# Four transformer blocks on one NeuronCore: the last block's cross attention scores issued three steps ahead, its exponentials placed behind weight copies

## The chip, the cores and the metric

One core of a Trainium2 chip runs the whole program in one launch. The metric is device time in microseconds; the time before is the median of three runs. The engines are TensorE (PE, with its weight loads shown as PEld), VectorE (DVE), ScalarE (ACT), GpSimd (POOL) and SyncE (SP, which issues the loads).

## What is computed

Eight sequences of 112 tokens of 256 features pass through four blocks; a context of 375 tokens of 192 features is shared by all cross attentions. Blocks L0 and L1 have self attention, cross attention and a gated feed-forward part, L2 has cross attention alone, L3 is a decoder layer. The last one matters most here (shortened):

```python
def _decoder_block(x, enc, tgt_mask, enc_mask, ...):   # 16 heads of 16 features
    h = _layernorm(x, ln1_w, ln1_b)
    qkv = (h @ qkv_w + qkv_b).reshape(B, T, 3, H, HD)
    attn = softmax(where(tgt_mask | causal, -inf, q @ k^T * scale))
    x = x + (attn @ v) @ proj_w + proj_b
    h = _layernorm(x, ln2_w, ln2_b)
    q, k, v = h @ q_w + q_b, enc @ k_w + k_b, enc @ v_w + v_b
    attn = softmax(where(enc_mask, -inf, q @ k^T * scale))
    x = x + (attn @ v) @ out_w + out_b
    h = gelu(_layernorm(x, ln3_w, ln3_b) @ mlp1_w + mlp1_b)
    return x + h @ mlp2_w + mlp2_b
```

Everything is float32. In L0 to L2 there are 16 heads of 64 features.

## The kernel before

**Stages and steps.** The ten parts of the four blocks are stages 0 to 9: 0 self, 1 cross, 2 feed-forward (L0); 3, 4, 5 the same (L1); 6 cross (L2); 7 self, 8 cross, 9 MLP (L3). Attention is cut into 176 *steps*, numbered in the order of execution. A self step takes eight heads of one sequence, a cross step four. Steps 0 to 47 are L0's, 48 to 95 L1's, 96 to 135 stage 6 with some steps of stage 7 between them. Stage 7 is woven in pairs of steps between sequences of stages 6 and 8 (132/133, 136/137, 142/143, 148/149 and 154/155 are the last pairs). Stage 8 starts at step 138; from 156 to 175 it runs without stage 7.

**A step's parts.** `add_step` makes these items for step s:

- `("S", s)`, `emit_s`: score matmuls into the PSUM pool `ps_s` (L986), and the first half of the softmax. `ps_s` has two tiles of two banks, and a step of stage 7 or 8 uses both. In stages 7 and 8 one DVE instruction per head adds the mask, takes the row extremum and moves the scores from PSUM to a probability tile `pr` (L934); an exponential per head follows on ACT in place (L942), with the row sum accumulated. In stages 1, 4 and 6 it is DVE maximum (L948), ACT exponential (L954), DVE reciprocal (L960) and a POOL multiply by the reciprocal per head (L963).
- `("E", s)`, `emit_late`, stages 7 and 8 only: the other half of the exponentials, kept in program order.
- `("T", s, k)`, `emit_t`: bank k of transposes of `pr` (L1013; three banks of four transposes in a cross step, two in a self step) into a tile of the PSUM pool `ps_m`, and its copy to a `wT` tile. In stages 7 and 8 the copy of bank 1 is on DVE (L1019), those of banks 0 and 2 on ACT (L1022). `ps_m` has four tiles in rotation, and every other matmul but the scores uses it too.
- `("PV", s)`, `emit_pv`: values (L1043) and their evacuation on DVE (L1054). They are issued for two steps at a time, every second iteration.
- for the last step of a sequence in stages 7 and 8, `("R", ...)` (reciprocal L1082, spread on POOL L1083) and `("N", ...)` (two transposes L1089, multiply L1091).

**Fillers.** All other work is planner items with a cost and a due time in steps: q/k projections of the last block (L725), values (L750), key jobs in two parts (`kj`: L791 begins them, L800 ends them), value jobs (`vj`: L866, L875 in the last block), output products with the next normalization (`norm`, L669), norm transposes (`hT`, L637), masks (`mask`, POOL), the last MLP's first product (`ff`, L1298) and its Gelu over a half of the result at a time (`gelu`, L1330). Projected q, k and v live in one SBUF tile, the *arena*, of 11300 columns; an item whose results find no room there waits. Weights come through a ring of seven buffers.

**Order.** TensorE's order is the order in which the items are issued. The main loop runs over iterations i: scores of step i+2, values (every second iteration), transposes of step i+1 with fillers between the banks, late exponentials of step i+2, fillers, and the first part of the next key or value job. On the other engines the instructions are ordered by a scheduler, except those that are marked `keep_in_program_order`. The interval of step n means the time from the start of its scores to the start of the scores of step n+1.

The main loop before:

```python
            if lo <= i + 2 < hi:
                plan.main(("S", i + 2))
            if lo <= i < hi:
                waiting.append(("PV", i))       # issued when two wait
            if lo <= i + 1 < hi:
                left -= plan.fill(2 * share, ...)
                for k in range(n):
                    plan.main(("T", i + 1, k))
                    left -= plan.fill(min(left, share))
            if ("E", i + 2) in plan.items and lo <= i + 2 < hi:
                plan.main(("E", i + 2))
```

Of the kernel before, what the change touches and what calls it, by code (L numbers as in the profile page):

```python
# [15 lines left out]
B, T, D = 8, 112, 256  # L16
S, DC = 375, 192
# [282 lines left out]
def kernel(ctx: ExitStack, tc: tile.TileContext, a: dict, out: bass.AP):  # L300
    nc = tc.nc
    PSUM = bass.MemoryType.PSUM
    RINGS = {"w": 7, "row": 2, "xn": 3}
    ARENA = 11300

    const = ctx.enter_context(tc.tile_pool(name="const", bufs=1))
    wpool = ctx.enter_context(tc.tile_pool(name="wpool", bufs=RINGS["w"]))
    rpool = ctx.enter_context(tc.tile_pool(name="rpool", bufs=RINGS["row"]))
    ppool = ctx.enter_context(tc.tile_pool(name="ppool", bufs=4))
    tpool = ctx.enter_context(tc.tile_pool(name="tpool", bufs=8))  # L310
    xpool = ctx.enter_context(tc.tile_pool(name="xpool", bufs=RINGS["xn"]))
    small = ctx.enter_context(tc.tile_pool(name="small", bufs=4))
# [8 lines left out]
    plan = Plan(RINGS, ARENA, lambda k: 512 if k[0] == "v" else S if k[0] == "k" and k[1] in (1, 4, 6, 8) else 4 * T)  # L321
# [7 lines left out]
    SEG = [0, 0, 0, 1, 1, 1, 2, 2, 2, 2]  # L329
# [216 lines left out]
    def add_masks():  # L546


        src = ("w", "m8")

        def load():
            m8 = wpool.tile([T, B * (T + S)], U8, tag="w", name="m8")
            nc.sync.dma_start(m8[:, : B * T], a["mask_BxS_bf0"].rearrange("b t -> (b t)").partition_broadcast(T))
            nc.sync.dma_start(m8[:, B * T :], a["mask_BxS2_bf0"].rearrange("b s -> (b s)").partition_broadcast(T))
            got[src] = m8

        def self_mask():
            nc.gpsimd.tensor_scalar_mul(cmask.rearrange("p b t -> p (b t)"), got[src][:, : B * T], NEG)
            nc.gpsimd.affine_select(
                cmask, cmask, pattern=[[0, B], [-1, T]], compare_op=ALU.is_ge, fill=NEG, base=0,  # L560
                channel_multiplier=1,
            )

        plan.add_load(Item(("load", "masks"), 0, load, makes=[src]))
        plan.add(Item(("mask", "self"), 0, self_mask, first_of(7, 0) - 8, uses=[src], seg=SEG[6]))
        yield
        for i in range(2):
            key = ("w", "cm", i)

            def place(i=i, key=key):  # L570
                got[key] = wpool.tile([T, 4, S], F32, tag="w", name="cm")

            plan.add_load(Item(("load", key), 0, place, makes=[key]))
            for n in range(4):

                def ctx_mask(i=i, n=n, key=key):
                    c = B * T + (4 * i + n) * S
                    nc.gpsimd.tensor_scalar_mul(got[key][:, n, :], got[src][:, c : c + S], NEG)

                b = 4 * i + n  # L580
                plan.add(Item(("mask", b), 0, ctx_mask, first_of(8, b) - 5, uses=[src, key], seg=SEG[7]))


    xns = {}
# [323 lines left out]
    steps = []  # L908
    at = {}
    norms = []  # L910
    bsums, pairs = {}, {}

    def add_step(st, b, blocks, dh, nk, qs, ks, qap, kap, vtile, mask, opos, ochunk, last=False, pair=None):

# [2 lines left out]
        s = len(steps)  # L917
# [3 lines left out]
        cell, late = {}, []  # L921
# [54 lines left out]
        def emit_s():  # L976
            if dh == 16 and (st, b) not in bsums:
                bsums[(st, b)] = small.tile([T, H], F32, tag="bsums", name="bsums")
            tiles = [ps_s.tile([T, 2, 512], F32, tag="s", name="s") for _ in blocks]

            order = [(i, n) for i, blk in enumerate(blocks) for n in range(len(blk))]
            if dh == 16:
                order.sort(key=lambda e: (e[1] // 2, e[0]))
            for i, n in order:
                h = blocks[i][n]
                nc.tensor.matmul(  # L986
                    tiles[i][:, n % 2, (n // 2) * nk : (n // 2 + 1) * nk], lhsT=qap(h), rhs=kap(h),
                    start=True, stop=True,
                )
            for i, blk in enumerate(blocks):  # L990
                pr = softmax(blk, tiles[i])
                for n, h in enumerate(blk):
                    cell[h] = pr[:, n % 2, n // 2, :]
            for _ in range(len(late) // 2):
                late.pop(0)()

        def emit_late():

            for exp in late:
                tc.keep_in_program_order(exp())  # L1000


        if nch == 1:
# [163 lines left out]
    def first_of(st, b):  # L1167
        return at[(st, b, 0)]
# [9 lines left out]
        return lambda t: [(("N", st, last_batch(t)), 1.2)]  # L1178

    def q_deadline(st, j):  # L1180
        return first_of(st, 2 * j) - 3.4

    L0 = ("L0_xattn_", "Wq1 Wk1 Wv1 Wo1 bo1 g1 b1 Wq2 Wk2 Wv2 Wo2 bo2 g2 b2 Wp Wf bf g3 b3 bp".split())
    L1 = (
# [24 lines left out]
    def hT_by(st):  # L1209
        if st == 9:  # L1210
            return lambda gi: last_of(8, last_batch(GROUPS[gi][-1])) + 2.0
        if st in ff_at:
            return lambda gi: ff_at[st] - 0.5 + 0.02 * gi
        return lambda gi: first_of(st, (256 * gi) // T) - 4

    def norm_by(st):
        f = hT_by(st)
# [19 lines left out]
    def cross_stage(st, wq, wk, wv, qscale, vscale):  # L1237
        last = st == 8
        for j in range(4):
            if last:  # L1240
                add_last_projection(st, "q", j, wq, ("sq", "qc"), q_deadline(st, j), 2)
            else:
                add_pair_projection(st, "q", j, wq, 4, lambda j, u: q_deadline(st, j) + 0.01 * u, qscale)
        for b in range(B):

            add_key_jobs(st, b, wk, lambda b, u: at[(st, b, u)] - 3.0, last)
            if not last:
                add_value_jobs(st, b, wv, lambda b, i: at[(st, b, (0, 0, 2)[i])] - 1.5 + 0.1 * i, vscale)

        if last:  # L1250
            add_last_values(st, wv, lambda b: first_of(st, b) - 1.3)
# [107 lines left out]
    st = 0  # L1359
# [82 lines left out]
    last_ff(9, w("m1"), L3 + "mlp1_b")  # L1442
    add_products(9, None, w("m2"), 8, after_last_ff(9), lambda t: f9 + 1 + 0.1 * t)


    plan.pump()
    for t in range(NT):
# [8 lines left out]
    nc.vector.tensor_copy(vcols, pt0[:, :NVR])  # L1456
    plan.now = 7.0

    cuts = [0, ff_at[2], ff_at[5], ff_at[9]]
    for seg in range(3):  # L1460
        lo, hi = cuts[seg], cuts[seg + 1]
# [14 lines left out]
        for i in range(lo - 2, hi):  # L1476
            plan.step = i
            left = plan.pace(i, seg)
            if i < lo:

                left = max(left, 6.5)
            plan.close_jobs()
            if lo <= i + 2 < hi:
                plan.main(("S", i + 2))


            if lo <= i < hi:
                waiting.append(("PV", i))
                full = 4 if seg < 2 and i < lo + 16 else 2
                if len(waiting) == full:  # L1490
                    while waiting:
                        plan.main(waiting.pop(0))
            if lo <= i + 1 < hi:
                n = steps[i + 1]
                share = left / (n + 2)
                left -= plan.fill(2 * share, 1.5 if i < lo else 0.0)
                for k in range(n):
                    plan.main(("T", i + 1, k))
                    left -= plan.fill(min(left, share))
            if ("E", i + 2) in plan.items and lo <= i + 2 < hi:  # L1500
                plan.main(("E", i + 2))
            plan.fill(left, 1.5 if i < lo else 0.0)


            plan.open_jobs(1 if i + 1 >= first_of(8, 0) or i + 2 in woven else 2, i + 3.5, seg)
# [38 lines left out]
```

## Time and profile before

| | |
|---|---|
| three runs | 1650.48, 1651.93, 1650.52 us; median 1650.52 |
| profiled execution | 1651.93 us, of which the span is 1650.1 |
| instructions in it | 30008 |
| mean granted TensorE clock | 0.999 |
| stage 8's first scores (step 138) | 1421.69 us |
| last scores (step 175) | 1597.85 us |
| last PE matmul starts | 1643.18 us |
| TensorE granted clock, 40 slices | 9 tenths or more in each |

Times are microseconds from the span's start. In rows of the timeline the columns are start, duration, engine, line, operation, output and inputs with their shapes, the number of instructions merged into the row, and in brackets how long the engine sat idle before it and what ended the wait. In the chain of waits a piece is start, duration, engine, tile and line. fp32 matmuls are recorded as two each: "x8" scores are four heads, "x48" values are two cross steps.

### The profile page before, as it was taken

Reading aid. Unit: us, or ns where it says so; the run is one execution under the profiler, and the core shown is the slowest. Engines: PE = TensorE matmul, PEld = TensorE weight load, DVE = VectorE, ACT = ScalarE, POOL = GpSimd, SP = SyncE. Lnnn points to the kernel's source line nnn. Section 1 sums busy time; section 2 is a strip of 40 time slices with the busy share of each in tenths; the row PEclk is TensorE's granted clock in tenths of the full one; section 3 lists DMA queues with packets and bytes.
Section 4 is the critical chain, followed back from the end, with each engine's and each line's share of the span. In section 5 each row is a group of like instructions: output and inputs, shape, how many; then the busy total and the mean of one; then the engine's idle time right before and its main releaser. Section 6 shows DMA issues by size and latency. Waiting matters only on the chain.

```text
span 1650.1 us, 30008 instructions
## 1 busy us (share of the span) xinstructions
PE 1631.5 (99%) x11772; PEld 1141.1 (69%) x11772; DVE 810.8 (49%) x2160; ACT 783.9 (48%) x2454; POOL 718.3 (44%) x687
## 2 busy tenths in 40 slices
PE   9999999999999999999999999999999999999999
PEld 8777766666657878666666665676666666766667
DVE  3544454545532244445444552345555556678762
ACT  3553444444531454434444452234445555777772
POOL 1323554655732223355565570364564447422110
PEclk9999999999999999999999999999999999999999
DMA  6020020000101011000000010100000000000000
GB/s 188 7 73 29 6 79 9 1 26 1 52 29 46 1 30 52 27 1 30 1 1 27 1 46 29 33 23 1 1 2 1 16 1 27 30 2 2 2 1 23
DMA packets 26611, 39.47 MB, mean 24 GB/s; under 512 B 1527, under 2 KB 21623, under 8 KB 26471
## 3 DMA queue, kind: packets, MB, share of 16 engines
q1 hardware_dynamic: 26231, 37.40, 7.2%
q8 instruction: 92, 1.51, 0.4%
q14 instruction: 48, 0.39, 0.1%
q10 hardware_dynamic: 240, 0.17, 0.0%
HBM read 35.88 MB, written 0.92 MB: 22 GB/s over the span
## 4 chain that ended last, share of the span: by engine, by line
PE 91%; ACT 3%; DVE 3%; POOL 1%; issue 1%; ACTq 0%; POOLq 0%; DVEq 0%
PE mm L669 13%; PE mm L703 11%; PE mm L1043 10%; PE s L986 10%; PE mm L1013 10%; PE mm L791 8%; PE mm L825 7%; PE mm L1263 6%; PE mm L800 5%; PE mm L834 4%; PE mm L750 3%; ACT pr L942 2%; PE mm L1298 2%; PE mm L637 1%; ACT pr L954 1%
## 5 line engine op out<-in xcount | busy, mean ns | idle before, releaser
L963 POOL TENSOR_SCALAR pr<-pr,rinv 112x375 f32<-112x375 f32 x384 | 468.7, 1239 | 331.9 <-DVE rinv L960 331.9
L954 ACT ACTIVATE pr<-s,nm 112x375 f32<-112x375 f32 (+1 forms) x640 | 301.9, 489 | 166.5 <-DVE nm L948 163.0
L355 DVE COPY arena<-mm 128x375 f32<-128x375 f32 (+4 forms) x187 | 112.4, 609 | 281.7 <-PE mm L800 138.3
L1013 PEld LDWEIGHTS mm<-ident,pr 112*128 112x128 f32 (+2 forms) x1920 | 209.6, 151 | 49.0 <-issue 21.3
L1013 PE MATMUL mm<-ident,pr 112*128 112x112 f32 (+2 forms) x1920 | 235.2, 264 | 4.6 <-ACT pr L942 2.6
L347 ACT COPY arena<-mm 128x375 f32<-128x375 f32 (+4 forms) x181 | 93.9, 519 | 302.6 <-PE mm L800 144.5
L948 DVE TENSOR_REDUCE nm<-s 112x2 f32<-112x750 f32 (+1 forms) x224 | 206.3, 957 | 52.9 <-PE s L986 49.4
L986 PE MATMUL s<-arena 64*112 64x375 f32 (+3 forms) x1792 | 211.1, 394 | 0.1
L1043 PEld LDWEIGHTS mm<-wT,arena 128*64 128x64 f32 (+5 forms) x3840 | 159.8, 129 | 36.3 <-issue 13.9
L1043 PE MATMUL mm<-wT,arena 128*64 128x112 f32 (+5 forms) x3840 | 177.7, 261 | 0.0
L347 ACT COPY wT<-mm 128x448 f32<-128x448 f32 (+2 forms) x224 | 117.8, 535 | 112.2 <-PE mm L1013 111.8
L986 PEld LDWEIGHTS s<-arena 64*112 64x112 f32 (+1 forms) x1792 | 114.3, 172 | 80.8 <-issue 31.8
L969 POOL TENSOR_TENSOR pr<-pr,rinv 112x896 f32<-112x896 f32 x32 | 53.9, 1684 | 202.2 <-DVE rinv L967 197.3
L942 ACT ACTIVATE pr<-pr,nm 112x112 f32<-112x112 f32 (+1 forms) x256 | 124.6, 490 | 30.5 <-DVE nm L934 30.5
L954 ACT ACTIVATION_READ_ACCUMULATOR pr<-s,nm 112x1 f32 x640 | 133.1, 208 | 0.0
L599 POOL TENSOR_TENSOR rs<-ve,mhalf 128x1 f32<-128x1 f32 x70 | 39.7, 568 | 197.5 <-DVE ve L597 197.3
L960 DVE RECIPROCAL rinv<-sums 112x1 f32<-112x1 f32 x384 | 62.4, 163 | 91.2 <-ACT pr L954 90.7
L825 PE MATMUL mm<-L_xattn_Wv,ctxA 128*128 128x512 f32 (+1 forms) x192 | 92.1, 602 | 2.1 <-ACT wT L347 1.3
L791 PE MATMUL mm<-ctxA,L_xattn_Wk 128*128 128x375 f32 x256 | 91.1, 482 | 1.1 <-DVE wT L355 0.9
L673 DVE TENSOR_TENSOR x<-mm,x 128x256 f32<-128x256 f32 x70 | 29.6, 423 | 119.0 <-PE mm L669 119.0
L355 DVE COPY wT<-mm 128x448 f32<-128x448 f32 (+2 forms) x128 | 78.2, 612 | 18.5 <-PE mm L1013 18.3
L703 PE MATMUL mm<-hT,L_xattn_Wq 128*128 128x224 f32 x384 | 83.1, 360 | 0.2 <-DVE wT L355 0.2
(134 smaller groups left out, 2293.2 us busy)
## 6 DMA issues: line engine op xcount, KB each, us to landing
L_xattn_Wo<-in_L_xattn_Wo_dram SPq DMA_DIRECT2D x3, 1024.0 KB, 15.0
L_xattn_w_ff<-in_L_xattn_w_ff_dram SPq DMA_DIRECT2D x3, 1024.0 KB, 5.2
L_xattn_Wv<-in_L_xattn_Wv_dram SPq DMA_DIRECT2D x4, 512.0 KB, 4.7
L_xattn_Wq<-in_L_xattn_Wq_dram SPq DMA_DIRECT2D x2, 1024.0 KB, 4.8
L_xattn_Wp<-in_L_xattn_Wp_dram SPq DMA_DIRECT2D x2, 1024.0 KB, 5.7
L_xattn_wq<-in_L_xattn_wq_dram SPq DMA_DIRECT2D x2, 1024.0 KB
L_xattn_wo<-in_L_xattn_wo_dram SPq DMA_DIRECT2D x2, 1024.0 KB, 5.3
L_xattn_mlp_w<-in_L_xattn_mlp_w_dram SPq DMA_DIRECT2D x2, 1024.0 KB, 5.2
```

Of the source, the lines that this page charges most:

```text
L347: nc.scalar.copy(dst, src)
L355: nc.vector.tensor_copy(dst, src)
L669: nc.tensor.matmul(ps[:, :D], lhsT=oT[:, c, t * P : (t + 1) * P], rhs=got[wv or w][:, c, :], start=(c == 0), stop=(c == n - 1),)
L703: nc.tensor.matmul(ps[:, i * 2 * T : (i + 1) * 2 * T], lhsT=got[w][:, k, m * P : (m + 1) * P], rhs=hT[:, k, lo:hi], start=(k == 0), stop=( ...
L791: nc.tensor.matmul(ps[:, :S], lhsT=got[wv][:, (2 * u + i) * P : (2 * u + i + 1) * P], rhs=ctxA[:, cols], start=True, stop=False,)
L825: nc.tensor.matmul(ps[: KCH[c][1], :], lhsT=lhs(ctxA, slice(0, KA), c), rhs=got[w][:, hf * 512 : (hf + 1) * 512], start=True, stop=False,)
L948: nc.vector.tensor_reduce(nm[:, :, :ns], sv, AX.X, ALU.max, negate=True)
L954: nc.scalar.activation(pr[:, bk, sl, :], sv[:, bk, sl, :], AF.Exp, bias=nm[:, bk, sl : sl + 1], accum_out=sums[:, bk, sl : sl + 1],)
L963: nc.gpsimd.tensor_scalar_mul(pr[:, bk, sl, :], pr[:, bk, sl, :], rinv[:, bk, sl : sl + 1])
L986: nc.tensor.matmul(tiles[i][:, n % 2, (n // 2) * nk : (n // 2 + 1) * nk], lhsT=qap(h), rhs=kap(h), start=True, stop=True,)
L1013: nc.tensor.transpose(pt[:kl, m * T : (m + 1) * T], cell[h][:, c * P : c * P + kl], ident[:T, :T])
L1043: nc.tensor.matmul(po[p0 : p0 + dp, blk * T : (blk + 1) * T], lhsT=got[vk][:kl, hv * dp : (hv + 1) * dp], rhs=wt, start=(c == 0 and par(h) ...
```

## The change

- From step 138 on, scores run three steps ahead: iteration i issues those of step i+3. At iteration 135, where this begins, those of 137 and 138 come together.
- In stage 8 the score item issues no exponential. Behind each bank's copy of step i+1 comes one exponential of the step whose scores this iteration issued (two if that is a self step, from step 138 on); the rest stays in the late item. All of stage 8's exponentials, and those of the self steps from 138 on, are then in program order.
- The pool of probability tiles has six buffers instead of four, and the arena 9536 columns instead of 11300.
- In the last two stages q projections, norm transposes, keys and masks are due one step earlier.

```diff
-    ARENA = 11300
+    ARENA = 9536
-    ppool = ctx.enter_context(tc.tile_pool(name="ppool", bufs=4))
+    ppool = ctx.enter_context(tc.tile_pool(name="ppool", bufs=6))
...
-            for _ in range(len(late) // 2):
+            for _ in range(0 if s >= first_of(8, 0) else len(late) // 2):
                 late.pop(0)()
+        def emit_some(n):
+            for _ in range(min(n, len(late))):
+                tc.keep_in_program_order(late.pop(0)())
         def emit_late():
-            for exp in late:
-                tc.keep_in_program_order(exp())
+            emit_some(len(late))
+        some[s] = emit_some
...
     def q_deadline(st, j):
-        return first_of(st, 2 * j) - 3.4
+        return first_of(st, 2 * j) - (4.4 if st > 6 else 3.4)
-        return lambda gi: first_of(st, (256 * gi) // T) - 4
+        return lambda gi: first_of(st, (256 * gi) // T) - (5 if st > 6 else 4)
-            add_key_jobs(st, b, wk, lambda b, u: at[(st, b, u)] - 3.0, last)
+            add_key_jobs(st, b, wk, lambda b, u: at[(st, b, u)] - (4.0 if last else 3.0), last)
...
+    def steps_heads(n):
+        return 4 * steps[n] if steps[n] == 2 else 4
+    DEEP = first_of(8, 0) - 3
...
-            if lo <= i + 2 < hi:
-                plan.main(("S", i + 2))
+            ahead = 3 if seg == 2 and i >= DEEP else 2
+            due = [n for n in range(i + 2, i + ahead + 1) if lo <= n < hi and not plan.items[("S", n)].done]
+            for n in due:
+                plan.main(("S", n))
...
                 for k in range(n):
                     plan.main(("T", i + 1, k))
+                    for m in due:
+                        if m >= first_of(8, 0):
+                            some[m](steps_heads(m) // 4)
                     left -= plan.fill(min(left, share))
-            if ("E", i + 2) in plan.items and lo <= i + 2 < hi:
-                plan.main(("E", i + 2))
+            for n in due:
+                if ("E", n) in plan.items:
+                    plan.main(("E", n))
```

The masks' due times move by one step in the same way (self mask from 8 to 9 steps before stage 7, context masks from 5 to 6 before their sequence).

More of the change, by code (lines that the diff above doesn't have):

```diff
@@ L564, in add_masks @@
         plan.add_load(Item(("load", "masks"), 0, load, makes=[src]))
-        plan.add(Item(("mask", "self"), 0, self_mask, first_of(7, 0) - 8, uses=[src], seg=SEG[6]))
+        plan.add(Item(("mask", "self"), 0, self_mask, first_of(7, 0) - 9, uses=[src], seg=SEG[6]))
         yield
@@ L580, in add_masks @@
                 b = 4 * i + n
-                plan.add(Item(("mask", b), 0, ctx_mask, first_of(8, b) - 5, uses=[src, key], seg=SEG[7]))
+                plan.add(Item(("mask", b), 0, ctx_mask, first_of(8, b) - 6, uses=[src, key], seg=SEG[7]))
     xns = {}
@@ L910 @@
     norms = []
-    bsums, pairs = {}, {}
+    bsums, pairs, some = {}, {}, {}
     def add_step(st, b, blocks, dh, nk, qs, ks, qap, kap, vtile, mask, opos, ochunk, last=False, pair=None):
```

## The prediction

> **What bounds the kernel now.** I read the page first, then the chain of waits, then busy time by windows, then the timeline of the last block. The page says TensorE:
>
> ```profile
> PE 1631.5 (99%) x11772; PEld 1141.1 (69%) x11772; DVE 810.8 (49%) x2160; ACT 783.9 (48%) x2454; POOL 718.3 (44%) x687
> ...
> PE 91%; ACT 3%; DVE 3%; POOL 1%; issue 1%; ACTq 0%; POOLq 0%; DVEq 0%
> ```
>
> The 8% of the chain off TensorE are the quarry. They lie near the end. In the windows by stage (columns: window, length, busy us of PE, PEld, DVE, ACT, POOL, granted clock, DMA share, GB/s):
>
> ```profile
> 1406.10:1597.85 191.75, 185.26 (x1998) 127.92 (x1997) 139.77 (x556) 144.28 (x468) 46.19 (x74) 0.99 0.03 8
> ...
> 1550.00:1597.85 47.85, 46.93 (x487) 30.56 (x479) 33.43 (x118) 36.07 (x101) 7.29 (x13) 1.00 0.01 2
> ```
>
> 1406.10 is the start of the scores of step 136, 1597.85 that of step 175, the last. DVE and ACT are busy 73% and 75%, so neither is the bound over the stretch. PE's 185.26 hides waits, because the ends are modelled. So I priced its work from unstalled pieces of the chain of waits:
>
> ```profile
> 1556.73 0.63 PE mm L875 x4
> ...
> 1567.61 0.80 PE mm L1013 x8
> ...
> 1570.52 0.83 PE s L986 x8
> 1571.35 1.29 PE mm L1043 x48
> 1572.64 1.91 PE mm L1298 x4
> ```
>
> That is: 0.40 per bank of transposes, 0.83 per score step, 1.29 for the values of two steps. The stretch holds 31 score steps of stage 8 (25.7), 8 of stage 7 at 0.59 (4.7), 109 banks (43.6), values 28 x 0.645 + 8 x 0.30 + 2 x 1.23 (22.9), 7 key jobs at 2.28 (16.0), 12 value pairs at 1.63 (19.6), 6 q/k projections at 1.62 (9.7), 3 self values at 0.95 (2.9), 5 MLP columns at 1.73 (8.7), 11 products of two chunks at 0.87 and one of eight, half-weighted, at 1.73 (11.3), 6 norm transposes at 0.50 (3.0), 12 scale transposes at 0.23 (2.8). Sum 170.8 (terms rounded). Against 191.75 that leaves **21.0 us in which PE waits**. The price list is good: the interval from step 168's scores to step 169's takes 7.77 by the trace and 7.77 by the list.
>
> Half of the idle sits in iterations without values. There the transposes of step n+1 come right behind scores n+2 and find their exponentials unfinished:
>
> ```profile
> 1512.37 0.61 ACT L942 ACTIVATE pr<-pr,nm 112x375 f32<-112x375 f32 x1
> ...
> 1512.66 0.77 PE L1013 MATMUL mm<-ident,pr 112*128 112x112 f32 x3
> ...
> 1512.97 0.59 ACT L942 ACTIVATE pr<-pr,nm 112x375 f32<-112x375 f32 x1
> ...
> 1513.71 0.32 PE L1013 MATMUL mm<-ident,pr 112*128 112x112 f32 x1 [0.28 <-ACT pr L942]
> ```
>
> Transpose by transpose PE walks at ACT's 0.59 us. The worst place, 3.6 us in one interval, also loses clock:
>
> ```profile
> 1458.33 1.12 PE L1013 MATMUL mm<-ident,pr 112*128 112x112 f32 x9 [0.28 <-ACT pr L942]
> ...
> 1459.93 2.00 PE L669 MATMUL mm<-squares,oT 128*128 128x256 f32 x4 [0.48 <-ACT wT L1022]
> ```
>
> L669 takes 0.87 elsewhere; the granted clock from 1460 to 1462 is 0.51. The excess, 1.1 there and 0.75 on the next L791, is 1.9 us of the 21.
>
> **The change, part by part.** No TensorE, POOL or SP instruction is added or removed (6960, 691 and 98 as built, both times); 7 evacuations pass from ACT to DVE, 7 x 0.6 = 4 us spread over 1650, behind 50% idle on both. Order is all that changes.
>
> *Scores three ahead, six probability buffers.* Transposes of step n+1 now find exponentials issued one whole iteration earlier, so the wait above goes. What is late next:
>
> (a) The two score buffers. Scores n+3 wait until DVE has masked step n+2: 0.83 + 0.2 + 4 x 0.467 + 0.1 = 3.0 us from scores to scores. The trace shows it:
>
> ```profile
> 1477.61 0.90 PE L986 MATMUL s<-arena 32*112 32x375 f32 x8
> ...
> 1479.63 1.82 PE L986 MATMUL s<-arena 32*112 32x375 f32 x8
> ```
>
> The second started, stuck and ended at 1481.45. In the changed order the PE work of intervals 139, 147, 151, 153, 157, 165 and 173 is 2.5, 2.9, 1.86, 2.9, 1.86, 2.03, 2.03, so 4.9 us stay. Behind the stuck scores stand the values and transposes, and DVE's copies behind those.
>
> (b) Waits not on exponentials (norm chain, scale transposes): single rows of 0.3 to 0.5, six to a few of them, 2.0.
>
> (c) Exponentials behind copies. ACT's queue becomes copy, two exponentials, copy, two exponentials (the middle bank's copy is DVE's). The copy of the third bank ends about 0.2 + 0.53 + 2 x 0.59 + 0.53 = 2.4 us after the first bank's transposes, where it stood 1.2 earlier; values need it 0.8 (two banks) + 0.83 + 1.1 = 2.7 after. The cover is 0.3 plus any filler. Without cover, 16 such iterations at 0.5 cost 8; with it 0. I take 2, nearer the covered end, since most of the iterations hold a filler of 0.5 or more.
>
> 4.9 + 2.0 + 2.0 = 8.9 of 21.0 stay: **gain 12.1**.
>
> *Entry.* Scores 137 and 138 come in one iteration. 138 waits for 8 maskings of 0.195: 0.59 + 0.2 + 1.56 + 0.1 less its own 0.59 of work, 1.9 on PE, ahead of values 134/135 and transposes 136. Bounds 0 (POOL's multiplies at 1404.18 to 1409.08 release those anyway) and 3.8 (clock lost too). **Cost 1.9.**
>
> *Exit.* The last scores go out one iteration earlier, so the planner finds the first Gelu ready early: it now stands on ACT ahead of bank 2 of step 174 and banks 0 and 2 of step 175. Before, it ran after all of them:
>
> ```profile
> 1612.51 1.28 ACT L1330 ACT_TABLE_LOAD   x1
> 1613.81 5.60 ACT L1330 ACTIVATE oT<-oT 128x2048 f32<-128x2048 f32 x4
> ...
> 1617.70 1.13 PE L669 MATMUL mm<-squares,oT 128*128 128x256 f32 x4 [0.68 <-DVE oT L1091]
> ```
>
> Two of the four, those of 2048 elements, are two thirds: 3.73. From the end of bank 0's transposes of step 174, ACT needs 0.2 + 0.53 + 1.28 + 3.73 + 0.53 = 6.3 until the copy of bank 2 frees a PSUM buffer; PE has 0.50 + 4 x 0.40 + 0.87 = 3.0 until it needs that buffer (four rotate; the fourth allocation after it is bank 2 of step 175). Stall 3.3, less the 0.68 above, which an output product now covers: 2.6. Bounds 0 and 2.6 + 1.9 (clock); I add half the clock. **Cost 3.5.** On the clock the Trainium skill (TensorE: Matmul & The Clock Gate, The HAM clock gate) wants about 3.4 us of idle before the clock halves; in the row above two or three waits, none over 0.5 us and 1.2 us together, preceded 0.51. By the rule the exit would cost 2.6, by the row 4.5. And the skill (ScalarE: Activation LUTs, What ACT_TABLE_LOAD costs) counts a drain of about 1.38 us after each table switch; the row has the Gelu 0.02 us behind the load, so by the rule the stall is 4.7, by the row 3.3. I go by the rows.
>
> *Smaller arena, due times one step earlier.* 9536 columns instead of 11300 forbid some early projections, and TensorE's order changes from step 2 on. In the four stages up to step 95 the work between scores stays above 5 us but for a few intervals, as before: 0. In steps 97 to 135 nine intervals fall under 5.2 us instead of three (smallest 3.6). A cross step's chain, scores to the last of four POOL multiplies, is 8.2 us (1393.31 to 1396.64 for scores, maximum, exponential and reciprocal, then 4.88 on POOL). It is mostly covered by the heavier neighbour; step 134 has 6.4 instead of 9.7. Bounds -2 (six buffers free DVE and ACT earlier) and 9 x 2.0 = 18; near the low end since only pairs of light intervals uncover it: **cost 1.0**. Masks one step earlier sit on POOL's idle 76% of that stretch; SP's loads keep their rings: 0.
>
> Sum: -12.1 + 1.9 + 3.5 + 1.0 = **-5.7 us**. The profiled execution took 1651.93 (span 1650.1, 1.8 around it), 1.4 over the median of 1650.52; a difference carries over to either. 1650.52 - 5.7 = **1644.8**.
>
> **Rivals.**
>
> *All but the score buffers' floor recovered* (0.25): ACT and DVE at three quarters speak for it, local bursts against. -16.1 + 1.9 + 2.5 = -11.7: 1638.8.
>
> *The vector engine's masks take over as the wait* (0.12): the 3.0 us floor plus (b) plus (c) uncovered, 4.9 + 2 + 8 = 14.9 stay, gain 6.1, eaten by 1.9 + 3.5 + 1.0: 1650.2. For it: DVE carries masks, one copy in three, values and norms. Against: over the stretch it is idle 52 us.
>
> *Slower: the smaller arena uncovers the softmax chain before the last block* (0.20). Place: transposes behind the nine light intervals of steps 97 to 135. Price 0.6 to 2.0 each; at 1.3, 11.7 us: 1650.5 - 6.7 + 11.7 = 1655.5. It decides from 0.74 each. Against: POOL is 55% busy there and the order alternates light with heavy.
>
> That the change does not do what it says I exclude: the built order shows scores n+3 ahead of transposes n+1 from step 138 on.
>
> **Chances.** Forecast 0.43. About 0.2% (3.3 us) can be told from no change. Faster: 0.40 of the forecast and 0.25. Same: 0.03 of it, 0.09 of the second rival, 0.02 of the third. Slower: 0.03 and 0.18. The forecast's own range, by (c) and the exit's bounds, is 1641 to 1648; the whole reaches from 1636 to 1652.
>
> **What would show it.** From scores 136 to 175 some 180 to 183 us instead of 191.75, no L1013 waiting on `pr L942`, score rows stretched by 1 us in intervals 151, 157, 165, 173; a PE gap of about 3 us before the last transposes, beside the Gelu; scores of 136 within 1.5 us of 1406.1. If they start later than 1409, the arena decides; if the stretch keeps its 190, the masks do.

## The result, and the profile after

The changed kernel takes 1662.56 us (median; 1662.02 to 1663.64), the kernel before 1650.53 beside it: ratio 1.007, 95% interval 1.006 to 1.008. It is 12 us slower, where 5.7 us faster had been forecast and 1652 was the top of the range.

The page of the changed kernel (busy time by engine, then the chain that ended last):

```profile
PE 1633.9 (98%) x11772; PEld 1143.1 (69%) x11772; DVE 820.1 (49%) x2167; ACT 777.6 (47%) x2447; POOL 718.3 (43%) x687
...
PE 89%; DVE 4%; ACT 4%; POOL 2%; issue 1%; ACTq 0%; DVEq 0%; POOLq 0%
```

The same matmuls; TensorE's share of the chain fell from 91% to 89%, and DVE, ACT and POOL have one point more each. The windows of the last block, from scores 136 to scores 175 and in four parts:

```profile
1412.22:1602.09 189.87, 181.45 (x1981) 125.50 (x1980) 140.33 (x557) 137.86 (x459) 46.57 (x74) 1.00 0.03 8
1412.22:1460.00 47.78, 43.73 (x461) 32.79 (x461) 31.16 (x145) 32.00 (x119) 18.40 (x25) 1.00 0.09 26
...
1555.00:1602.09 47.09, 46.82 (x498) 30.04 (x496) 34.05 (x118) 33.10 (x96) 7.23 (x13) 1.00 0.01 2
```

Two of the prediction's own signs decide here. Scores 136 start at 1412.22 (0.9 of the 6.1 us stand already at the first scores of all), later than the 1409 from which "the arena decides". And the stretch keeps its 190 (189.87 against 191.75), from which "the masks do". It even holds less work than before, since scores 175 now go out one iteration earlier (1981 matmul records against 1998); so stretches are compared below only within one order.

Now TensorE's transposes, scores and value jobs of that block, by line. Before (busy us, mean ns, then idle time ahead of them and who ended it), from 1406 to 1599, which is from the scores of 136 to the end of those of 175:

```profile
L1013 PE MATMUL mm<-ident,pr 112*128 112x112 f32 (+2 forms) x438 | 56.2, 266 | 3.4 <-ACT pr L942 2.6 <-DVE oT L1054 0.3 <-POOL pr L963 0.2
L986 PE MATMUL s<-arena 32*112 32x375 f32 (+1 forms) x384 | 35.6, 439 | 0.1
L866 PE MATMUL mm<-ctx_w,ctxA 128*128 128x256 f32 (+1 forms) x48 | 13.3, 396 | 0.9 <-ACT wT L1022 0.9
```

After, from 1412 to 1603, the same score steps:

```profile
L1020 PE MATMUL mm<-ident,pr 112*128 112x112 f32 (+2 forms) x427 | 51.9, 265 | 1.3 <-POOL pr L963 0.9 <-DVE hT L642 0.4
L986 PE MATMUL s<-arena 32*112 32x375 f32 (+1 forms) x384 | 38.6, 439 | 1.4 <-DVE nm L934 1.3
L866 PE MATMUL mm<-ctx_w,ctxA 128*128 128x256 f32 (+1 forms) x48 | 13.5, 397 | 4.0 <-ACT wT L1029 2.0 <-DVE wT L1026 1.2 <-DVE x L673 0.6
```

The change did what it says: no transpose waits for `pr L942` any more, and they are 4.3 us less busy (some 1.4 of it because eleven fewer are recorded in the stretch). But the same number of score matmuls is 3.0 us longer (38.6 against 35.6) and waits 1.4 instead of 0.1; the entry, shown below, is 0.76 and 1.06 of that. And the value jobs (L866) wait 4.0 us instead of 0.9, for PSUM banks that copies on ACT and DVE still read. A row that is longer at the same mean of one instruction (439 ns) holds a stall inside. The timeline of PE and DVE in the changed kernel shows who causes it:

```profile
1486.51 0.90 PE L986 MATMUL s<-arena 32*112 32x375 f32 x8
...
1487.44 0.55 DVE L934 CUSTOM_DVE_ANT_0 pr<-s,cm 112x375 f32<-112x375 f32 x1
...
1487.92 0.54 DVE L934 CUSTOM_DVE_ANT_0 pr<-s,cm 112x375 f32<-112x375 f32 x1
...
1488.38 0.54 DVE L934 CUSTOM_DVE_ANT_0 pr<-s,cm 112x375 f32<-112x375 f32 x1
1488.52 1.82 PE L986 MATMUL s<-arena 32*112 32x375 f32 x8
...
1488.85 0.54 DVE L934 CUSTOM_DVE_ANT_0 pr<-s,cm 112x375 f32<-112x375 f32 x1
...
1489.32 0.39 DVE L1098 TENSOR_TENSOR oT<-mm,oT 128x224 f32<-128x224 f32 x1
1489.62 0.62 DVE L1026 COPY wT<-mm 112x448 f32<-112x448 f32 x1
1490.16 0.54 DVE L934 CUSTOM_DVE_ANT_0 pr<-s,cm 112x375 f32<-112x375 f32 x1
```

The scores of 1486.51 are masked one head at a time until 1489.4; the next scores start at 1488.52 in that one of the two score buffers which is already free, and stick until the second is (row of 1.82 where 0.90 is usual). VectorE goes from masking to a multiply, to a copy and to the next masking without a gap. The scores of 152, 158, 166 and 174 are stretched like this, by 0.8 to 0.9 us each, in the intervals that the prediction named.

### The profile page after: what moved, and what is told of

The parts are those of the page before. It is cut to its first block, busy times and chain, and to the rows that moved or that the text cites. A ratio compares the mean times of both kernels' runs of the same rounds, so it can differ in the third digit from the quotient of the medians.

```text
span 1660.2 us, 30180 instructions
## 1 busy us (share of the span) xinstructions
PE 1633.9 (98%) x11772; PEld 1143.1 (69%) x11772; DVE 820.1 (49%) x2167; ACT 777.6 (47%) x2447; POOL 718.3 (43%) x687
## 4 chain that ended last, share of the span: by engine, by line
PE 89%; DVE 4%; ACT 4%; POOL 2%; issue 1%; ACTq 0%; DVEq 0%; POOLq 0%
PE mm L669 12%; PE mm L703 11%; PE mm L1050 10%; PE s L986 10%; PE mm L1020 9%; PE mm L791 8%; PE mm L825 7%; PE mm L1270 6%; PE mm L800 5%; PE mm L834 4%; PE mm L750 3%; PE mm L1305 2%; DVE pr L934 1%; ACT pr L942 1%; ACT pr L954 1%; PE mm L725 1%
## 5 line engine op out<-in xcount | busy, mean ns | idle before, releaser
L963 POOL TENSOR_SCALAR pr<-pr,rinv 112x375 f32<-112x375 f32 x384 | 468.6, 1238 | 335.0 <-DVE rinv L960 335.0
L986 PE MATMUL s<-arena 64*112 64x375 f32 (+3 forms) x1792 | 214.7, 395 | 1.9 <-DVE nm L934 1.3
L942 ACT ACTIVATE pr<-pr,nm 112x112 f32<-112x112 f32 (+1 forms) x256 | 125.1, 494 | 6.4 <-DVE nm L934 6.4
L353 DVE TENSOR_SCALAR arena<-mm 128x448 f32<-128x448 f32 (+2 forms) x61 | 39.5, 648 | 93.1 <-PE mm L834 55.7
```

Of the source, the lines that this page charges most:

```text
L963: nc.gpsimd.tensor_scalar_mul(pr[:, bk, sl, :], pr[:, bk, sl, :], rinv[:, bk, sl : sl + 1])
L986: nc.tensor.matmul(tiles[i][:, n % 2, (n // 2) * nk : (n // 2 + 1) * nk], lhsT=qap(h), rhs=kap(h), start=True, stop=True,)
```

## The experiments

Each ratio is that of one kernel to the kernel before, run beside it. The kernels of the b and e groups (without e1), c4 and the two floors keep the TensorE order of the kernel in brackets; the others move scores or the planner's fillers, as told.

**Where the whole preparation stands.** Three parts of the change alone, and the exit:

```diff
 a1_arena (before)
-    ARENA = 11300
+    ARENA = 9536
 a2_due (before): the five due times one step earlier, as in the change
 a3_prep (before): a1 and a2, and
-    ppool = ctx.enter_context(tc.tile_pool(name="ppool", bufs=4))
+    ppool = ctx.enter_context(tc.tile_pool(name="ppool", bufs=6))
 a4_gelu (after), the Gelu item's dependences
-                    ... + [(("S", len(steps) - 1), 4.0)],
+                    ... + [(("T", len(steps) - 1, 2), 0)],
```

> The kernel before with one number changed: ARENA 9536 in place of 11300. If the smaller arena is what makes the changed kernel's scores of step 136 start 6.1 us late (1412.2 against 1406.1), this kernel loses 3 to 5 us against before: 1653.5 to 1655.5. The rival: the arena costs nothing and the late start comes from the due times or from the six probability buffers: 1649.5 to 1651.5.

> The kernel before with only the five due times of the last block one step earlier (arena 11300, four probability buffers, scores two ahead). If the arena is the cost, this one is within 1.5 us of before: 1649.5 to 1652. The rival: earlier due times fill the steps of stage 6 unevenly and are themselves the cost of 1.8 to 5 us between step 96 and step 136: 1652.5 to 1655.5.

> Everything of the change except the three-ahead scores and the exponentials' new place: arena 9536, six probability buffers, due times one step earlier. TensorE's order is that of the changed kernel up to the entry, and after it only the scores stand one iteration later. If the preparation costs the 5 to 6 us read off at step 136 and the three-ahead scores then lose another 6 (entry 4, last block -3, exit 4), this kernel takes 1655 to 1657, with scores of 136 at 1411 to 1412.5. The rival: the late start at 136 is harmless since the last block catches up, and the three-ahead scores cost all 12: 1649.5 to 1652.

> The changed kernel with the first two Gelus held until the last transposes, so that on ACT they stand behind all copies of weights, as in the kernel before; nothing else moves. If the Gelu among the copies costs what the tail shows (0.58 + 1.82 us of waiting and 1.9 us of halved clock against 0.68 before), this kernel gains 2.5 to 4 us: 1658.5 to 1660. The rival: the Gelus then end later by as much, and the output products that follow wait for them: 1661.5 to 1663.

| kernel | median, us | ratio to before, 95% interval |
|---|---|---|
| a1_arena | 1656.23 | 1.0033 (1.0022 to 1.0044) |
| a2_due | 1655.57 | 1.0026 (1.0017 to 1.0035) |
| a3_prep | 1658.60 | 1.0041 (1.0027 to 1.0055) |
| a4_gelu | 1659.53 | 1.0050 (1.0037 to 1.0062) |

The arena alone costs 5 us, the due times 4, where the first expectation had none for these and its rival was right; together with the buffers they cost 6.8 (0.0041 x 1651), a little more than expected. The six buffers alone were not run. So more than half of the 12 us is lost without a single score being issued earlier. The held Gelu gains 0.0020 x 1651 = 3.3, as expected. One place where the small arena loses time, PE's timeline in a1_arena:

```profile
1368.73 0.32 PE L1013 MATMUL mm<-ident,pr 112*128 112x112 f32 x1 [0.70 <-POOL pr L963]
...
1369.94 1.61 PE L1013 MATMUL mm<-ident,pr 112*128 112x112 f32 x9 [0.90 <-POOL pr L963]
```

and the same place in its windows (the column before the last two is the granted clock):

```profile
1368.00:1370.00 2.00, 0.40 (x3) 0.20 (x3) 1.37 (x4) 1.65 (x6) 2.00 (x3) 1.00 0.00 0
1370.00:1372.00 2.00, 2.00 (x10) 1.69 (x11) 1.10 (x3) 1.21 (x5) 2.00 (x2) 0.60 0.00 0
1372.00:1374.00 2.00, 2.00 (x4) 0.78 (x3) 0.29 (x2) 0.00 (x0) 2.00 (x3) 0.55 0.00 0
```

The transposes find POOL still multiplying, wait 1.6 us in two pieces, and then pay 0.8 + 0.9 = 1.7 for a clock of 0.60 and 0.55: a single light interval for 3.3 us. In the kernel before no transpose waits for `pr L963` between 1100 and 1406. The clock's part is not paid each time: the executions of a1 with a mean clock of 1.000 took 1654.88 and 1655.44 us, those with 0.997, the profiled one among them, 1658.04 to 1659.50.

The exit, PE and ACT of the changed kernel:

```profile
1613.08 1.28 ACT L1337 ACT_TABLE_LOAD   x1
...
1614.37 3.71 ACT L1337 ACTIVATE oT<-oT 128x2048 f32<-128x2048 f32 x2
...
1616.06 0.67 PE L1020 MATMUL mm<-ident,pr 112*119 112x112 f32 x4 [0.58 <-DVE oT L1314]
...
1617.99 1.38 ACT L1029 COPY wT<-mm 119x448 f32<-119x448 f32 x3
1618.55 5.41 PE L1305 MATMUL mm<-hT,L_xattn_mlp_w 128*128 128x256 f32 x16 [1.82 <-ACT wT L1029]
```

and the same TensorE row with the Gelu held, in a4_gelu:

```profile
1616.26 3.63 PE L1305 MATMUL mm<-hT,L_xattn_mlp_w 128*128 128x256 f32 x16
```

Three copies queue behind the Gelus; TensorE waits 0.58 us for an evacuation on VectorE and 1.82 us for the PSUM bank of one of the copies. Its next row takes 5.41 instead of 3.63, and there the clock of the changed kernel is halved:

```profile
1618.00:1620.00 2.00, 1.45 (x4) 1.22 (x5) 0.00 (x0) 1.37 (x4) 0.00 (x0) 0.71 0.00 0
1620.00:1622.00 2.00, 2.00 (x6) 1.55 (x6) 0.48 (x1) 0.00 (x0) 0.00 (x0) 0.50 0.00 0
```

**What exponentials and their place are worth.**

```diff
 b1_copyfirst (after)
-                    for m in due:
-                        if m >= first_of(8, 0):
-                            some[m](steps_heads(m) // 4)
 b3_half (before, with emit_some of the change)
                     plan.main(("T", i + 1, k))
+                    if first_of(8, 0) <= i + 2 < hi:
+                        some[i + 2](2 if steps[i + 2] == 2 else 1)
 b4_noexp (before) and b5_noexp3 (after)
-NEG = -1.0e30
+NEG = -1.0e3
-                            pr, pr, AF.Exp, bias=nm, scale=-1.0, accum_out=...
+                            ex if s >= 136 else pr, pr[:, :8] if s >= 136 else pr, AF.Exp,
+                            bias=nm if s < 136 else 0.0, scale=-1.0 if s < 136 else 0.0, accum_out=...
```

> The changed kernel with all exponentials of the last block behind the iteration's copies of transposed weights, instead of one behind each copy; TensorE's order is the same. If the waits of the changed kernel (TensorE waiting 0.9 to 1.2 us for a PSUM bank that a copy on ACT or DVE holds) come from exponentials standing ahead of copies, this kernel gains 2 to 4 us over the changed one: 1658.5 to 1660.5. The rival: the score buffers and DVE's maskings set the pace, and it does not matter where ACT puts its copies: 1662 to 1663.5. Should the exponentials become late again, with transposes waiting on them, 1664 or more.

> The kernel before (scores two ahead, arena 11300, four buffers, old due times), in which only the second half of each step's exponentials moves: from behind the last copy of the iteration to behind the first and second. If the 0.27 to 0.6 us waits of transposes on exponentials are the part of the idle time that can be had, this kernel has them without the smaller arena: 1647.5 to 1649.5. The rival: the last copy comes 1.2 us later, values and PSUM banks wait for it instead, and nothing is gained: 1650.5 to 1653.

> The kernel before, with the exponentials of the last block's steps from 136 on left out but for 8 of their columns, written to a scratch tile, so that no transpose waits for one and ACT is about half as busy; the masked scores are transposed as they are (with a mask value of -1000 so that all stays finite). TensorE's order and work are those of before. If the prediction's 21 us of idle time between the scores of 136 and of 175 are real and 12 of them hang on exponentials, the stretch falls from 191.75 to 178 to 181 us. The rival: the price list counted real work as waiting, the waits that rows show add up to about 12 of which 8 hang on exponentials: 183 to 186 us, total 1643 to 1647.

> The changed kernel with the same exponentials left out in the same way (8 columns, scratch tile, mask value -1000). What it gains over the changed kernel is what exponentials still cost there. If they hold up the copies and so the PSUM banks, the stretch from the scores of 136 to those of 175 falls from 189.9 by 4 to 8 us and the total to 1652 to 1658. The rival: the waits left are those for DVE's maskings and the score buffers: it falls by less than 3 us, total 1659 to 1662.

| kernel | median, us | ratio to before, 95% interval |
|---|---|---|
| b1_copyfirst | 1663.09 | 1.0080 (1.0068 to 1.0093) |
| b3_half | 1651.95 | 1.0005 (0.9997 to 1.0014) |
| b4_noexp | 1647.59 | 0.9980 (0.9971 to 0.9989) |
| b5_noexp3 | 1658.56 | 1.0047 (1.0033 to 1.0060) |

b4 is the one that overturns the forecast. With no exponential left to wait for, the kernel before gains 3.3 us, and its stretch falls to 187.14, not to the 178 to 181 of the prediction's picture or the 183 to 186 of its rival. Twelve microseconds were not there to be had from exponentials. (Its transposes still wait for the maskings of their own step.) b5 takes 3.8 us less than the changed kernel (0.0023 x 1651), just below the range of its rival, while its stretch falls by 2.6, as that rival had it. The two orders of ACT's queue (b1, b3) gain nothing.

**Entry, exit and the two halves of the small arena's cost.**

```diff
 c1_entry (after): the second of two due score steps goes behind values and fillers
-            for n in due:
+            for n in due[:1]:
                 plan.main(("S", n))
 ...
                 left -= plan.fill(2 * share, 1.5 if i < lo else 0.0)
+                for m in due[1:]:
+                    plan.main(("S", m))
 c2_both (after): c1 and a4
 c3_early (before)
-    plan = Plan(RINGS, ARENA, ...
+    plan = Plan(RINGS, 9536, ...
+        if seg == 2:
+            plan.arena = ARENA
 c4_order (before): the edit of b3, and as in the change
-            for _ in range(len(late) // 2):
+            for _ in range(0 if s >= first_of(8, 0) else len(late) // 2):
```

> The changed kernel with one step moved: where three-ahead begins, the second score step (138) stands behind the values and the value projection of that iteration instead of right behind scores 137; nothing else on TensorE moves. If the entry's cost is the wait of scores 138 for the eight maskings of 137 (rows: 1.06 us of idle and 0.76 of stretch), this gains 1.5 to 2.5 us over the changed kernel: 1660 to 1661. The rival: whatever is late at the entry waits a little further on for the same maskings or copies, and nothing is gained: 1662 to 1663.5.

> The changed kernel with both repairs, the entry's second score step moved and the Gelus held behind the last copies. If entry and exit add up, 1657 to 1658.5, which is the kernel with the preparation alone (1658.6) or at most 1.5 us better: three-ahead itself would then be worth 0 to 1.5 us. The rival, the prediction's own picture of 12 us to be had in the block: that they stay hidden behind something else that goes with these two, and the kernel falls below 1654.

> The kernel before with the planner held to 9536 columns until the third segment (step 96) and to 11300 from there on: TensorE's order is that of the kernel with the small arena up to the end of the second segment and that of before from there. The prediction put the small arena's cost up to step 95 at 0. If that holds, 1650.5 to 1651.5 and the whole cost of the small arena (5 us) lies in stage 6. The rival, by the start of scores 44 (2.8 to 3.1 us late with the small arena): 1653 to 1655.

> The second part of the change alone, on the kernel before: scores two ahead, arena and buffers as before, but none of the last block's exponentials at the scores, one behind each copy of a bank and the rest behind the last. If the place of the exponentials matters only where scores are two ahead, the last exponential now ends 0.6 to 1.2 us later in each iteration without values, about 8 of them: 1654 to 1659. The rival: as with three ahead, ACT's order costs nothing because TensorE waits for banks and score buffers instead: 1650 to 1652.

| kernel | median, us | ratio to before, 95% interval |
|---|---|---|
| c1_entry | 1659.02 | 1.0052 (1.0039 to 1.0064) |
| c2_both | 1656.17 | 1.0033 (1.0020 to 1.0046) |
| c3_early | 1653.24 | 1.0015 (1.0006 to 1.0023) |
| c4_order | 1656.29 | 1.0030 (1.0019 to 1.0041) |

Entry and exit add up: c1 gains 0.0018 (3.0 us), a4 0.0020, both 0.0037. What c1 removes stands in the changed kernel's timeline of PE:

```profile
1419.32 0.66 PE L986 MATMUL s<-arena 32*112 32x112 f32 x16
1421.04 1.66 PE L986 MATMUL s<-arena 32*112 32x375 f32 x8 [1.06 <-DVE nm L934]
```

and in c1_entry the same scores, now behind the values, run through:

```profile
1418.50 0.66 PE L986 MATMUL s<-arena 32*112 32x112 f32 x16
...
1422.60 0.90 PE L986 MATMUL s<-arena 32*112 32x375 f32 x8
```

These rows are 1.06 + 0.76 = 1.8 us of the 3.0; the other 1.2 has no row in this profile. In the profile of a4_gelu, which keeps the old entry, the same wait of 1.06 and the same row of 1.66 stand, and behind them the clock is low:

```profile
1422.00:1424.00 2.00, 2.00 (x32) 2.00 (x28) 1.10 (x6) 0.00 (x0) 0.00 (x0) 0.60 0.02 4
1424.00:1426.00 2.00, 2.00 (x21) 1.72 (x19) 0.00 (x0) 0.11 (x1) 0.71 (x3) 0.55 0.00 0
```

That is another 1.7 us. In the changed kernel's own profile the clock is 1.00 there, so the same entry cost 1.8 us in one profiled execution and 3.5 in the other.

c3 says that 0.0015 (2.5 us) of the small arena's 0.0033 is lost before step 96. c4 says that having all exponentials behind copies, none with the scores, costs 5 us when scores are only two steps ahead; b3, which keeps the first half with the scores, costs nothing that can be told.

**What is left when no softmax is in the way.** b4's stretch of 187.14 left 16 us over the priced work. The next kernels cut the maskings too, to 8 columns, and let the transposes read a constant; d3 tries another preparation.

```diff
 d1_floor (before) and d2_floor3 (after): b4's edit, and for steps from 136 on
-                        pr[:, bk, sl, :], sv[:, bk, sl, :], mask(), -1.0, ...
+                        pr[:, bk, sl, :w8], sv[:, bk, sl, :w8], mask()[:, :w8], -1.0, ...
+                        cell[h] = cmask.rearrange("p b t -> p (b t)")[:, :nk]
 d3_nodue (c2_both): the five due times as in before
```

> The kernel before with the softmax of steps 136 to 175 cut to 8 columns on VectorE and ScalarE, and the transposes reading a constant mask tile, so that they wait for no part of a softmax and score buffers come free at once. TensorE's order and work are those of before. If the price list was right (170.8 us) and the rest are waits for maskings and score buffers, the stretch from scores 136 to 175 falls from 191.75 to 172 to 175 us. If the list left out work, 178 to 184 us: then that much of the 21.0 us was never idle.

> The changed kernel with the softmax cut in the same way. Against the changed kernel without exponentials alone (1658.6) it shows what maskings and score buffers cost in the three-ahead order. If they took the place of the exponentials as the wait, it falls by 4 to 6 us: 1652.5 to 1654.5. The rival: TensorE waits in that order for PSUM banks and the norm chain, which stay: 1656.5 to 1658.5.

> The changed kernel with entry and exit repaired and the five due times of the kernel before. If the due times' cost (4.3 us alone, about 2 on top of the small arena) goes with them and three-ahead itself is worth 1.3 us, it takes the small arena's 1656.2 less 1.3: 1654 to 1655.5. The rival: without the shift, projections come too late for scores three ahead, are forced in front of them and lose what is won: 1656 to 1659.

| kernel | median, us | ratio to before, 95% interval |
|---|---|---|
| d1_floor | 1637.54 | 0.9917 (0.9903 to 0.9930) |
| d2_floor3 | 1647.71 | 0.9979 (0.9970 to 0.9988) |
| d3_nodue | 1653.35 | 1.0016 (1.0007 to 1.0025) |

The windows of the stretch in b4_noexp:

```profile
1405.62:1592.76 187.14, 181.61 (x1997) 127.02 (x1996) 139.12 (x555) 100.02 (x468) 45.84 (x74) 1.00 0.03 8
```

and in d1_floor:

```profile
1406.80:1584.45 177.65, 176.69 (x1997) 124.99 (x1996) 92.59 (x556) 100.39 (x468) 45.88 (x74) 1.00 0.03 9
```

ACT's column (100) is the same in both; VectorE's fell from 139.12 to 92.59, and 9.5 us of waiting went with it. In the order of the change, b5_noexp3 and d2_floor3 against 189.87:

```profile
1411.08:1598.39 187.31, 182.03 (x1982) 126.71 (x1981) 140.93 (x557) 92.34 (x462) 46.33 (x74) 0.99 0.03 8
1411.91:1589.41 177.50, 174.57 (x1982) 123.73 (x1981) 92.85 (x557) 92.05 (x462) 46.26 (x74) 1.00 0.03 9
```

That is 2.6 and 9.8 us, but b5's profiled execution lost some 1.7 to a low clock at the entry (0.76, 0.50 and 0.89 in the windows of 2 us from 1420 to 1426), which the other two did not, so 4.3 and 8.1 as well. Likewise 1.9 of the 4.6 in the order of before is the clock lost there at 1460, which b4 does not lose. So in either order exponentials hold 3 to 5 us and maskings, with the score buffers and all that VectorE does behind them, 8 to 10. The medians say the same of the whole kernel: 3.3 and 4.0 for exponentials, 10.1 and 10.9 for maskings. The maskings were taken away after the exponentials; no kernel leaves out maskings alone, so how the two would share in that order isn't shown. d2 fell almost 5 us below the lowest time expected of it: the maskings' share had been put too low once more.

d3 takes 2.8 us less than a1, whose arena and due times it shares (it has six probability buffers where a1 has four); c2 takes 1.3 less than a3, 2.4 by the medians. The due times aren't needed.

**Three steps ahead without a preparation.** The last block's every third score step keeps its probabilities in the end of the arena, which the planner gives up from step 133 on, when nothing lies there any more.

```diff
 e1_tail (d3_nodue)
-    ARENA = 9536
+    ARENA = 11300
+    KEEP = 9536
-                    end = lo
+                    end = min(end, lo)
-    ... name="ppool", bufs=6))
+    ... name="ppool", bufs=4))
+            if s >= first_of(8, 0) and s % 3 == 0:
+                lo = KEEP + 882 * blocks.index(blk)
+                pr = arena[:T, lo : lo + 2 * ns * nk].rearrange("p (b s k) -> p b s k", b=2, s=ns)
+            else:
+                pr = ppool.tile([T, 2, ns, nk], F32, tag="pr", name="pr")
 ...
+            if i >= 133:
+                plan.arena = KEEP
 e2_act (e1_tail) and e3_act2 (before)
-                nc.vector.tensor_copy(wt[:kl, :n], pt[:kl, :n])
+                (nc.scalar.copy if s >= first_of(8, 0) else nc.vector.tensor_copy)(wt[:kl, :n], pt[:kl, :n])
```

> Three steps ahead without its preparation: arena 11300, four probability buffers, the due times of before; every third score step of the last block (138, 141 and so on) keeps its probabilities in the last 1764 columns of the arena, which the planner gives up only from step 133 on. Entry and exit are repaired. TensorE's order equals that of before up to the entry. If the preparation is what costs 5 to 7 us and three-ahead is worth 1.3 to 2.8, this kernel is faster than before by that: 1648 to 1649.8. The prediction's 12.1 us would give 1639. The rival: the gains seen on the small arena came from its own disorder, and nothing is gained here: 1650.5 to 1653.

> The same kernel, with the middle bank's copy of each step of the last block on ACT too, so that VectorE has 0.6 us less a step between its maskings and ACT 0.53 more. If maskings on a busy VectorE are the wait, it gains 2 to 4 us over the other: 1645 to 1647.5. The rival: ACT's queue of exponentials and three copies becomes the wait: 1650 to 1655.

> The kernel before with only the middle bank's copy moved to ACT. With scores two ahead the transposes wait for exponentials on ACT, which now stand behind one more copy: 1651.5 to 1655. The rival: earlier maskings outweigh it: 1648 to 1650.

| kernel | median, us | ratio to before, 95% interval |
|---|---|---|
| e1_tail | 1648.51 | 0.9985 (0.9976 to 0.9994) |
| e2_act | 1655.28 | 1.0026 (1.0016 to 1.0035) |
| e3_act2 | 1653.12 | 1.0013 (1.0005 to 1.0022) |

e1 is faster than both kernels, by 2.5 us against before. That is what three steps ahead, with entry and exit repaired, are worth by themselves. Freeing VectorE at ACT's expense loses 2 us in the old order and 6.8 in the new one: ACT has no more room than VectorE.

## Why the prediction was wrong

The parts as measured, in us (ratios times 1651, each uncertain by 1.5 to 3):

| term | predicted | measured | by |
|---|---|---|---|
| three steps ahead in the block | -12.1 | -1.3 (-2.8 and -2.5 on other preparations) | a3 to c2; a1 to d3; before to e1 |
| entry | +1.9 | +3.0 | after to c1 |
| exit | +3.5 | +3.3 | after to a4 |
| arena, buffers, due times | +1.0 | +6.8 | before to a3 |
| sum | -5.7 | +11.8 | the whole change: +12.0 |

**The 21.0 us of idle time.** The first step that failed. In d1 almost nothing of a softmax is waited for, and the stretch still takes 177.65 us, with 1.0 us of waits in its rows: TensorE's work is about 176.7, not 170.8. Added up in d1's timeline from the start of each row to the start of the next, the output products take 13.8 us where the list has 11.3, the transposes 45.8 where it has 43.6, and the values 24.3 where it has 22.9. The largest single piece is found in the timeline of before, the last product of the stage ahead, which the list has "half-weighted, at 1.73":

```profile
1416.24 3.63 PE L669 MATMUL mm<-L_xattn_Wo,oT 128*128 128x256 f32 x16
```

So about 15 us were lost (191.75 - 176.7), the 1.9 of clock among them.

**The gain of 12.1.** The step that cost most. It was the remainder after (a), (b) and (c), which makes exponentials responsible for all that isn't priced otherwise. Measured, exponentials hold 4.6 us of the stretch (clock included) and maskings with the score buffers 9.5: most of the idle time belonged to a wait that the change leaves as long as it was (8 to 10 us after). The mechanism of (a) was right, and so were the place and nearly the size of the stuck scores: outside the entry their rows are 3.9 us longer and wait 0.2, where 4.9 was priced. What was mis-sized is the rest that hangs on the queues of VectorE and ACT. (c) gave 2.0 to late copies, but the value jobs alone wait 4.0 us for them, 0.9 before (1.8 in b5, 0.9 in d2); and what stands behind the stuck scores was named without a price. In the rows of 1486 to 1490 VectorE has a multiply and the middle bank's copy between its maskings. What three-ahead takes from the transposes (4.3 us less busy, 2.9 at equal number) the scores take back (3.0 more).

Of (c) itself, exponentials ahead of copies: putting all copies first gains nothing with three steps ahead (b1: 0.5 us slower by the medians, 1.7 by the ratios, within the error); with two ahead, all of them behind copies cost 5 us (c4).

**Entry and exit.** Entry: the wait was right (1.9 priced, 1.8 in the rows); what was missing is the halved clock in some executions, which stood in its upper bound. Exit: the mechanism was right, the stall behind the Gelu and the clock, but the sum of 3.5 was met by luck. The stall was priced at 2.6 and is 0.58 + 1.82 - 0.68 = 1.7 in the rows; the clock was taken at half of 1.9 and cost 5.41 - 3.63 = 1.8 in this execution. Of the two rules of the Trainium skill weighed there, the drain (ScalarE: Activation LUTs, What ACT_TABLE_LOAD costs) isn't seen here either: the Gelu starts 0.01 us behind the end of the table load (1614.36). And the clock fell after waits of 0.58 and 1.82 us with work between them, where the other (TensorE: Matmul & The Clock Gate, The HAM clock gate) asks for 3.4 us of idle; the row decides.

**The preparation.** "In the four stages up to step 95 [...] 0" was wrong: 2.5 us are lost there (c3). For steps 97 to 135 the prediction had the mechanism, light intervals uncovering POOL's chain, and gave it to its slower rival; a1's row shows it, 1.6 us of waiting and 1.7 of clock in one place. The value was taken near the low end of bounds from -2 to 18, on the ground that only pairs of light intervals uncover the chain. The due times, which had no price of their own, cost 4 us alone.

**The rivals.** Both that were given little were right in kind: maskings are the wait (0.12), though they were so before the change already and did not take over, and the smaller arena lost time ahead of the block (0.20), in part before step 96, where that rival did not look. Each was priced as if the other didn't happen. With 6.1 gained (second rival) and 11.7 lost (third), the same sum gives 1650.5 - 6.1 + 1.9 + 3.5 + 11.7 = 1661.5. That it comes near 1662.56 is luck: measured, 1.3 to 2.8 were gained and 6.8 lost.

**What stays open.** Where exactly the small arena loses its 2.5 us before step 96, and the due times their 4: in the profiles these are differences of the scores' start times between steps 16 and 44, and after step 104, without one row that holds them. Whether score buffers or VectorE's queue is the harder limit of the maskings wasn't taken apart: no kernel had more score buffers. What six probability buffers cost or gain by themselves wasn't run either.

## What to carry to other kernels

Idle time that is left over after pricing the work has no owner yet: before promising it to an edit, take the suspected wait away altogether and see what the kernel gains; here one such kernel (b4) would have said 3.3 us where 12.1 were forecast, and 1.3 to 2.8 were found. An edit that needs memory is charged for the plan that loses it, over the whole kernel, and that can cost more than the edit brings; room that is free only where it is needed (e1) made the difference between 2.6 us slower (d3) and 2.5 us faster. When work is issued earlier, look at what its being done early releases: here a Gelu that moved ahead of three copies.

## What had not been expected of the hardware

TensorE's clock halved behind short waits with work between them: 0.70 + 0.90 us (a1, up to 1369.94) and 0.58 + 1.82 us (after, up to 1618.55) were each followed by 4 us in which the windows show 0.50 to 0.71, worth 1.7 and 1.8 us, about as much as the waits. A wait does not always bring it: the entry shows 0.60 and 0.55 behind its 1.06 us in a4 and 1.00 in after, so a price for such a wait has two values.
